# Two halves of 64 tokens solved in turn inside a chunk, the first clears on another queue, and a new order of turns

## The chip, the cores and the metric

The kernel runs on one core of a Trainium2 chip. Five engines work side by side, each with its own instruction stream that is executed in order: TensorE (PE: products and transposes, results into PSUM), VectorE (DVE), ScalarE (ACT), GpSimd (POOL) and SyncE (SP, which here only issues DMAs). The metric is the device time of one execution in microseconds; of several executions the median counts.

## The reference

The program is one layer in three parts on an input of 2 sequences x 4096 tokens x 256 features. All is float32.

```
x = x + 0.5 * ffn(layernorm(x))       # 8 experts, the best 2 of each token
x = x + attn(layernorm(x))
x = x + 0.5 * ffn(layernorm(x))
```

The expert part computes logits, a softmax over 8 experts, takes the two best, scales the token by each score, and adds `(silu(xs @ w1[e]) * (xs @ w3[e])) @ w2[e]` over those experts.

The attention has 4 heads of 64 and is a gated delta rule. For each chunk of tokens, with the state S carried from chunk to chunk:

```
A   = I + tril(Kb @ K.T, -1)          # Kb = K * beta
T   = inverse(A)                      # lower triangular
mid = T @ Vb - (T @ Kb) @ S.T
O   = Q @ S.T + (Q @ K.T * M) @ mid   # M: lower triangular ones
S   = S + mid.T @ K
```

Chunks of any length give the same result; the reference uses 64 tokens, the kernel 128. In block form, with A cut in two halves of 64, the low half of mid is T_ll r_l, and the high half is T_hh (r_h - A_hl mid_l), where r is the right side before T is applied. The change is about these two ways to get mid.

## The kernel before

**The units.** The tokens are cut in 16 units of 512 (256 of each sequence). The first expert layer handles them in groups of 1, 3, 4, 4, 4 units, the second in groups of 4, 4, 4, 3, 1. A group of one unit ("dense") runs all experts on all its tokens (`weigh`, `all_experts`). The other groups sort tokens by expert: `route` finds scores and slots, `scatter` puts each scaled token row into the DRAM buffer `slots` by an indirect DMA on GpSimd, `experts` reads pairs of 128-row tiles from `slots` (tile `xi`), runs the selected expert and stores to `made` (tile `yo`), and `combine` gathers two rows a token from `made`. There are two `slots` buffers, used by the groups in turn, of 40 tiles of 128 rows at most. Rows that no token takes must be finite, so `clear` (line 707) writes zeros into each buffer once, 8 tiles (1 MB) a DMA, from the zeroed tile `XT[1]` (4 KB a partition before it takes its first real content).

**Attention.** `project` makes k, q and v of a unit (products `pj`, a short convolution in `cv`). `gram` makes the matrix L = K K.T of a chunk of 128 tokens for 8 pairs of sequence and head, and stores its four diagonal blocks of 32 to DRAM. `substitute` inverts all 32-blocks of four chunks (128 rows at once) on VectorE, and stores the inverses X and their transposes. `inverse` (line 1359) puts the inverse of a chunk together:

- it loads the four 32-blocks of the transposed inverse into the diagonal of `xt` and three blocks of the inverse into `xx`, seven DMAs on SyncE;
- it joins blocks of 32 to blocks of 64 in both halves at once: products `pp`, negated copy `pm`, products `px`, copies back to `xt`; for the low half the untransposed corner is made as well (the third loop of `px`, copied into `xx`);
- it joins the two blocks of 64 to one of 128: products `pq` (L's corner times the high block), negated copy `pw`, products `pz` (times the low block), and a copy into the corner of `xt`.

`advance` (line 1409) then makes the masked product `at`, the transposed k (`kt`) and r; takes `pks` = K S off r; forms `pmid` = T r as eight products with 128 rows and 128 columns of weights; copies it to `mid`; and from mid makes the output `po` and the step of the state `pds`, which is added to S. `finish` normalises the output, applies Wo and stores. There are 32 chunks, one behind the other through S.

**PSUM.** Four rings of two banks: "fa" (projection, first expert products), "tr" (transposes), "at" (all of `inverse`, `gram` and `pa`), and "y" (`pks`, `pmid`, `po`, `pds`, the experts' second product `py`, and small ones). The tiles of a ring are handed out in the order of the program text.

**The order.** Nothing is issued while the program text runs: every operation is noted in `Plan.ops` with a cost, and `Plan.order` (line 432) then lays out all operations engine by engine with those costs. Among ready operations an engine takes the one with the lowest `first` value, which is the operation's number plus an entry of `TURNS` (line 47; one integer for a step of the program, a few thousand at most). `plan.together()` makes one operation of several products. `nc.either.copy` leaves it to this layout whether VectorE or ScalarE copies. `plan.hold` makes an operation wait, in this layout only, for a given earlier one. What is laid out becomes the real in-order streams of PE, DVE, ACT and SP. A `yield` in the program text ends a step and tells its estimated share.

**The head.** The first DMAs load x for the first unit, the experts' weights and further x. The second group (three units, `groups[1]`) gets its `slots` cleared by four DMAs on ScalarE's queue (line 1065) without a hold; the attention's weights follow on SyncE, held until `groups[0].last`, the operation that completes the dense group's weights `wt`. The other groups' clears (six DMAs) are on SyncE, held until `groups[1].last`.

Of the kernel before, what the change touches and what calls it, by code (L numbers as in the profile page):

```python
# [36 lines left out]
F32 = mybir.dt.float32  # L37
# [3 lines left out]
ALU = mybir.AluOpType  # L41
# [6 lines left out]
    0: -503, 1: -513, 2: -516, 3: -370, 4: -583, 5: 726, 6: -2518, 7: -130, 8: -302, 9: 87,  # L48
    10: -124, 11: -210, 12: -120, 13: -49, 14: -31, 16: 37, 17: 151, 18: 3947, 19: 159, 20: 180,
    21: 1716, 22: 88, 23: -235, 24: -40, 25: 1464, 26: 884, 27: 1522, 28: 483, 29: 1766, 30: 2462,  # L50
    31: 2582, 32: 3382, 33: 170, 34: -217, 35: 428, 36: -1592, 37: 115, 38: 51, 39: 255, 40: 643,
    41: -669, 42: -210, 43: -509, 44: 505, 45: -127, 46: 91, 47: 1585, 48: 38, 49: 1295, 50: 193,
    51: 1197, 52: 216, 53: -416, 54: 1088, 55: -982, 56: -953, 57: -958, 58: -1515, 59: -1356,
    60: -824, 61: -627, 62: -312, 63: -308, 64: -221, 65: -302, 66: -280, 67: -44, 69: -15,
    70: -62, 71: -145, 72: -50, 73: -46, 74: -1795, 75: -55, 76: -9, 77: 1, 78: 364, 79: 100,
    80: -128, 81: 123, 82: 108, 83: 111, 84: -136, 85: -35, 86: 81, 87: 3, 88: 209, 89: 883,
    90: -104, 91: -82, 92: -14, 93: -22, 94: 222, 95: 298, 96: 1362, 97: 420, 98: -2033, 99: 760,
    100: -48, 101: 25, 102: -85, 103: -2631, 104: -2008, 105: -27, 106: -111, 107: -2148,
    108: 1154, 109: -39, 110: -3637, 111: -2138, 112: -1132, 113: -2221, 114: 21, 115: -1517,
    116: -206, 117: -1803, 118: -1354, 119: -431, 120: -706, 121: 262, 122: -274, 123: -46,  # L60
    124: -191, 125: -192, 126: 422, 127: 1624, 128: 282, 129: 476, 130: -367, 131: 348,
    132: -1154, 133: -780, 134: 44, 135: -614, 136: -460, 137: -333, 138: 67, 139: -480,
    140: -469, 141: -1054, 142: -358, 143: -626, 144: 622, 145: -369, 146: -360, 147: -255,
    148: 396, 149: -432, 150: -147, 151: -170, 152: -32, 153: -7, 154: -43, 156: -10, 157: 68,
# [487 lines left out]
def kernel(  # L552
# [488 lines left out]
    def prepare(g):  # L1041
# [16 lines left out]
        for i in range(n):  # L1058
# [5 lines left out]
            if g is groups[1]:  # L1064
                clear(g.par, upto, nc.scalar)
                if i == 0:
                    plan.hold = groups[0].last
                    load_attention()
                    plan.hold = None
# [623 lines left out]
```

## Time and profile before

| | us |
|---|---|
| median of 9 executions | 1844.44 |
| lowest, highest | 1836.61, 1853.97 |
| the profiled execution's own time | 1850.08 |
| its span, first to last instruction | 1848.3 |
| PE busy | 1627.6 |
| VectorE busy | 1237.4 |
| ScalarE busy | 754.5 |
| GpSimd busy | 702.3 |
| first product of a chunk (`pp`) starts | 386.6 |
| last step of the state (`pds`) ends | 1718.3 |
| bytes moved | 259.48 MB, 140 GB/s in the mean |

How to read the lines of a profile: "L202 PE MATMUL pmid<-r,XT 128*128 128x64 f32 x512 | 69.7, 294 | 15.4 <-..." is a group of instructions: source line (L202 is a helper that records the operation, so the tile names tell which it is), engine, operation, output and inputs, weights' rows*columns, the moving operand's shape, the number; then busy us of all, ns of one; then the idle time of the engine just before them and what ended it. A float32 product leaves two records, so 512 are 8 products in each of 32 chunks. Suffixes a and b name the first and second expert layer's tiles or, in the attention, a unit's. In a timeline the first two numbers are start and length in us; a bracket tells idle time before and what released it. ACTq, SPq and POOLq are the issues of DMAs by ScalarE, SyncE and GpSimd. "PE" busy counts modelled ends of pipelined products; "PEld" are weight loads.

### The profile page before, as it was taken

How to read it: one execution, taken by the hardware profiler on the slowest of the kernel's cores; microseconds unless marked ns; L12 is line 12 of the kernel's file. 1: busy time of each engine (PE TensorE's matmuls, PEld its weight loads, DVE VectorE, ACT ScalarE, POOL GpSimd, SP SyncE). 2: the span in 40 equal slices, each digit the busy share in tenths (PEclk: the TensorE clock that was granted, in tenths of full speed). 3: DMA queues.
4: the chain of work that ended last, by engine and by line, in shares of the span. 5: the costliest groups of instructions: out<-in, count | busy, mean ns of one | idle time of the engine just before them, and what ended most of it. 6: DMA issues, size and time to landing. Idle time of an engine off the chain costs nothing.

```text
span 1848.3 us, 34449 instructions
## 1 busy us (share of the span) xinstructions
PE 1627.6 (88%) x11656; PEld 1234.3 (67%) x11656; DVE 1237.4 (67%) x4166; ACT 754.5 (41%) x1566; POOL 702.3 (38%) x800
## 2 busy tenths in 40 slices
PE   3978789689989989999999899789899989999898
PEld 2656466567667667667677677657676767777776
DVE  3637568775785786587956867876875868376344
ACT  1425435333343535343544435343443533334432
POOL 2413744453112322642333362332215423454434
PEclk9999989888999989998999999899899998999999
DMA  7173564554133235643332562342145535574774
GB/s 239 55 281 115 174 213 144 185 166 125 54 91 91 79 94 159 175 135 110 112 95 87 162 178 92 107 122 68 46 136 170 162 115 161 175 223 157 219 222 120
DMA packets 296396, 259.48 MB, mean 140 GB/s; under 512 B 117536, under 2 KB 275232, under 8 KB 296224
## 3 DMA queue, kind: packets, MB, share of 16 engines
q1 hardware_dynamic: 271552, 190.13, 34.0%
q0 software_dynamic: 23040, 62.95, 10.4%
q10 hardware_dynamic: 1632, 4.21, 0.6%
q8 instruction: 96, 1.57, 0.4%
q14 instruction: 76, 0.62, 0.1%
HBM read 137.52 MB, written 119.67 MB: 139 GB/s over the span
## 4 chain that ended last, share of the span: by engine, by line
PE 44%; DVE 20%; DMA 17%; issue 9%; ACT 5%; POOL 4%; SPq 2%; POOLq 0%; DVEq 0%; ACTq 0%
PE pj_a L202 5%; PE po L202 4%; DVE cv_a L202 4%; DMA got_b<-made,sli_b 3%; DMA got_a<-made,sli_a 3%; PE pb_a L202 3%; PE p_b L1109 3%; PE p_a L1109 3%; PE pmid L202 2%; POOL slots L934 2%; DMA slots<-row_a,sli_a 2%; PE py_a L1109 2%; DMA slots<-row_b,sli_b 2%; PE pyo L202 2%; PE py_b L1109 2%
## 5 line engine op out<-in xcount | busy, mean ns | idle before, releaser
L202 DVE SCALAR_TENSOR_TENSOR cv_a<-pre_a,cw_sb,cv_a 128x512 f32<-128x512 f32 x288 | 212.2, 744 | 7.2 <-ACT cv_a L223 3.8
L202 PE MATMUL pj_a<-xT_a,wp_sb 128*128 128x512 f32 x384 | 195.3, 612 | 8.0 <-DVE xT_a L217 3.1
L934 POOL DMA_INDIRECT slots<-row_b,sli_b x120 | 120.8, 1007 | 192.7 <-DVE sli_b L202 78.0
L1109 PE MATMUL p_a<-wx_sb,xiT_a 128*128 x608 | 160.2, 401 | 17.6 <-ACT xiT_a L218 8.0
L934 POOL DMA_INDIRECT slots<-row_a,sli_a x120 | 120.8, 1007 | 116.0 <-issue 39.1
L952 POOL DMA_INDIRECT got_b<-made,sli_b x120 | 117.1, 975 | 118.1 <-DMA made<-yo_b 21.4
L1109 PE MATMUL p_b<-wx_sb,xiT_b 128*128 x608 | 155.5, 389 | 5.7 <-ACT xiT_b L218 2.1
L952 POOL DMA_INDIRECT got_a<-made,sli_a x120 | 123.1, 1026 | 83.5 <-DVE x_a_1c L202 17.9
L1109 PEld LDWEIGHTS p_a<-wx_sb,xiT_a 128*128 128x128 f32 x608 | 115.5, 200 | 48.9 <-ACT xiT_a L218 14.3
L1109 PEld LDWEIGHTS p_b<-wx_sb,xiT_b 128*128 128x128 f32 x608 | 109.5, 191 | 28.7 <-ACT xiT_b L218 7.5
L1109 PE MATMUL py_a<-wx_sb,hT_a 128*128 x304 | 85.9, 403 | 10.9 <-DVE hT_a L217 4.6
L202 PEld LDWEIGHTS pj_a<-xT_a,wp_sb 128*128 128x128 f32 x384 | 64.8, 192 | 41.4 <-issue 23.9
L202 POOL TENSOR_TENSOR rs_a<-ve_a,mhalf 128x4 f32<-128x4 f32 x32 | 33.9, 1060 | 152.0 <-DVE ve_a L202 151.8
L202 POOL TENSOR_TENSOR rr<-ms,mhalf 128x8 f32<-128x8 f32 x32 | 54.4, 1699 | 93.3 <-DVE ms L202 93.0
L1109 PE MATMUL py_b<-wx_sb,hT_b 128*128 x304 | 85.0, 400 | 3.4 <-DVE hT_b L217 1.0
L202 PE MATMUL po<-mid,at 128*128 128x64 f32 x512 | 85.2, 296 | 3.2 <-DVE at L202 1.7
L202 POOL COPY pre_a<-carry 128x6 f32<-128x6 f32 x96 | 28.3, 296 | 156.2 <-DVE cv_a L202 132.5
L202 DVE TENSOR_TENSOR yb<-yb,z 128x31 f32<-128x31 f32 (+15 forms) x248 | 84.0, 339 | 4.5
L202 PEld LDWEIGHTS po<-mid,at 128*128 128x128 f32 x512 | 81.1, 224 | 8.0 <-ACT mid L218 3.9
L202 DVE TENSOR_TENSOR z<-lb,yb 128x31 f32<-128x31 f32 (+15 forms) x248 | 83.4, 336 | 4.2
L202 POOL COPY carry<-pre_a 128x6 f32<-128x6 f32 x96 | 28.3, 302 | 150.2 <-ACT pre_a L218 140.4
L202 PE MATMUL pmid<-r,XT 128*128 128x64 f32 x512 | 69.7, 294 | 15.4 <-issue 6.5
(290 smaller groups left out, 3877.9 us busy)
## 6 DMA issues: line engine op xcount, KB each, us to landing
xi_a<-slots SPq DMA_DIRECT2D x76, 256.0 KB
made<-yo_a SPq DMA_DIRECT2D x76, 256.0 KB
xi_b<-slots SPq DMA_DIRECT2D x76, 256.0 KB
made<-yo_b SPq DMA_DIRECT2D x76, 256.0 KB
x_a<-in_L_attn_x_dram SPq DMA_DIRECT2D x32, 256.0 KB
x_a<-mid SPq DMA_DIRECT2D x16, 512.0 KB
xr<-mid SPq DMA_DIRECT2D x64, 128.0 KB
mid<-xr SPq DMA_DIRECT2D x64, 128.0 KB
```

Source lines behind the costliest of these rows:

```text
L202: self.plan.add(self.name, lambda: real(*args, **kw), ins, outs, cost)
L934: ins = tc.nc.gpsimd.indirect_dma_start(out=dst, out_offset=bass.IndirectOffsetOnAxis(ap=slot, axis=0), in_=row, in_offset=None,)
L952: return tc.nc.gpsimd.indirect_dma_start(out=got, out_offset=None, in_=src, in_offset=bass.IndirectOffsetOnAxis(ap=slot, axis=0),)
L1109: return tc.nc.tensor.matmul(o, lhsT=lhsT, rhs=wx_sb.rearrange("p e c -> p (e c)")[:, cols], start=start, stop=stop,)
```

## The change

Four things are changed together.

1. `inverse` stops at blocks of 64. The products `pq` and `pz`, the third loop of `px`, and the copies `pw`, `XT<-pz` and `X<-px` go; one of the seven loads goes. The tiles `XT` and `X` are half as wide, as they hold the two blocks of 64 below each other.
2. `advance` applies the two blocks in turn: the low half of `mid` from the low half of r, then the product `pl` of L's corner with it, which is taken off the high half of r on VectorE, then the high half of `mid`. Each is a group of eight products of 64 rows by 64 columns of weights with 64 moving columns. `pl` and the second `pmid` take tiles of the "y" ring. L is read here and no longer in `inverse`, so six instead of four tiles of L are kept.
3. All clears are issued by SyncE; those of the second group are held until the first group's weights are complete, as the attention's weights are. The zeros come from a tile of half the width, so a row of a clear is 2 KB and no longer 4 KB.
4. `TURNS` is another table (1003 entries for steps 0 to 1022, where there were 1020 for 0 to 1054, since each of the 32 `inverse` calls has one step fewer). The mean size of an entry is 1141 where it was 617, the largest 7426 where it was 3947.

```diff
 TURNS = {
-    0: -503, 1: -513, 2: -516, 3: -370, 4: -583, 5: 726, 6: -2518, 7: -130, 8: -302, 9: 87,
...
+    1017: -173, 1019: -53, 1020: 16, 1021: -506, 1022: -372,
 }
...
-    XT = [const.tile([P, NH, P], F32, name=f"XT_{i}") for i in range(2)]
-    X = [const.tile([P, NH, 2 * XB], F32, name=f"X_{i}") for i in range(2)]
+    XT = [const.tile([P, NH, 2 * XB], F32, name=f"XT_{i}") for i in range(2)]
+    X = [const.tile([P, NH, XB], F32, name=f"X_{i}") for i in range(2)]
...
-    def clear(i, upto, engine):
+    def clear(i, upto):
         for t in range(cleared[i], upto, 8):
             n = min(8, upto - t)
-            engine.dma_start(
-                slots[i][t * P : (t + n) * P, :].rearrange("(p c r) d -> p c (r d)", p=P, r=4),
-                XT[1].rearrange("p h c -> p (h c)").unsqueeze(1).to_broadcast([P, n // 4, NH * P]),
+            nc.sync.dma_start(
+                slots[i][t * P : (t + n) * P, :].rearrange("(p c r) d -> p c (r d)", p=P, r=2),
+                XT[1].rearrange("p h c -> p (h c)").unsqueeze(1).to_broadcast([P, n // 2, NH * 2 * XB]),
             )
...
-            if g is groups[1]:
-                clear(g.par, upto, nc.scalar)
-                if i == 0:
-                    plan.hold = groups[0].last
-                    load_attention()
-                    plan.hold = None
-            else:
-                plan.hold = groups[1].last
-                clear(g.par, upto, nc.sync)
-                plan.hold = None
+            plan.hold = groups[0 if g is groups[1] else 1].last
+            clear(g.par, upto)
+            if g is groups[1] and i == 0:
+                load_attention()
+            plan.hold = None
...
-        l = blk.tile([P, BP, 2, P], F32, tag="L", name=f"L_{n}_{t}", bufs=4)
+        l = blk.tile([P, BP, 2, P], F32, tag="L", name=f"L_{n}_{t}", bufs=6)
...
-        xt, xx, l = XT[t % 2], X[t % 2], Ls.pop((n, t))
+        xt, xx, l = XT[t % 2], X[t % 2], Ls[n, t]
         for c in range(NC):
             s = ts(t * NC + c, NH)
             nc.sync.dma_start(
-                xt[ts(c, XB), :, ts(c, XB)], XTd[n % 2][s, :].rearrange("q (r c) -> r q c", c=XB)
-            )
-            if c < 3:
+                xt[ts(c, XB), :, ts(c % 2, XB)],
+                XTd[n % 2][s, :].rearrange("q (r c) -> r q c", c=XB),
+            )
+            if c % 2 == 0:
...
-                    mm(px[a][fst[a], q, :], xx[fst[a], q, 0:XB], pm[fst[a], q, :])
-            for q in range(NH):
-                mm(px[0][snd[0], q, :], pm[fst[0], q, :], xx[fst[0], q, 0:XB])
-        nc.either.copy(xx[snd[0], :, 0:XB], px[0][snd[0]])
+                    mm(px[a][fst[a], q, :], xx[fst[a], q, :], pm[fst[a], q, :])
         for a in range(2):
-            nc.either.copy(xt[fst[a], :, snd[a]], px[a][fst[a]])
+            nc.either.copy(xt[fst[a], :, XB:], px[a][fst[a]])
         yield 3.0
-        lo, hi = slice(0, 2 * XB), slice(2 * XB, P)
-        pq = ps.tile([P, NH, 2 * XB], F32, tag="at", name=f"pq_{v}")
-        with plan.together():
-            for q in range(NH):
-                mm(pq[lo, q, :], l[hi, q, lo], xt[hi, q, hi])
-        pw = wk.tile([2 * XB, NH, 2 * XB], F32, tag="pw", name=f"pw_{v}", bufs=1)
-        nc.either.copy(pw, pq[lo], -1.0)
-        pz = ps.tile([P, NH, 2 * XB], F32, tag="at", name=f"pz_{v}")
-        with plan.together():
-            for q in range(NH):
-                mm(pz[lo, q, :], xx[lo, q, :], pw[:, q, :])
-        nc.either.copy(xt[lo, :, hi], pz[lo])
-        yield 2.0
...
-        pmid = ps.tile([P, NH, D], F32, tag="y", name=f"pmid_{v}")
-        with plan.together():
-            for h in range(NH):
-                mm(pmid[:, h, :], XT[t % 2][:, h, :], r[:, h, :])
+        xt, l = XT[t % 2], Ls.pop((n, t))
+        lo, hi = slice(0, 2 * XB), slice(2 * XB, P)
         mid = wk.tile([P, NH, D], F32, tag="mid", name=f"mid_{v}", bufs=1)
-        nc.either.copy(mid, pmid)
+        for s in (lo, hi):
+            if s == hi:
+                pl = ps.tile([P, NH, D], F32, tag="y", name=f"pl_{v}")
+                with plan.together():
+                    for h in range(NH):
+                        mm(pl[hi, h, :], l[lo, h, hi], mid[lo, h, :])
+                nc.vector.tensor_tensor(r[hi], r[hi], pl[hi], ALU.subtract)
+            pmid = ps.tile([P, NH, D], F32, tag="y", name=f"pmid_{v}_{s.start}")
+            with plan.together():
+                for h in range(NH):
+                    mm(pmid[s, h, :], xt[s, h, :], r[s, h, :])
+            nc.either.copy(mid[s], pmid[s])
```

## The prediction

> **What bounds the kernel now.** I read the page first, then a table of four stages (cut at the first and the last instruction of the chunks' products), then the groups by shape, then the timeline of single chunks and of the head.
>
> ```profile
> PE 1627.6 (88%) x11656; PEld 1234.3 (67%) x11656; DVE 1237.4 (67%) x4166; ACT 754.5 (41%) x1566; POOL 702.3 (38%) x800
> PE 44%; DVE 20%; DMA 17%; issue 9%; ACT 5%; POOL 4%; SPq 2%; POOLq 0%; DVEq 0%; ACTq 0%
> ```
>
> PE is the busiest engine, yet the chain of waits that ended last lies on it for 44% only, so I look stage by stage (columns: busy us of PE, PEld, DVE, ACT, POOL; granted clock; DMA share; GB/s).
>
> ```profile
> 0.00:100.00 100.00, 65.87 (x283) 47.08 (x284) 49.09 (x265) 29.80 (x73) 34.38 (x55) 0.98 0.41 143
> 100.00:377.00 277.00, 221.40 (x1040) 159.14 (x1039) 182.34 (x775) 117.79 (x248) 122.00 (x135) 0.93 0.58 189
> 377.00:1720.00 1343.00, 1227.32 (x9777) 939.17 (x9778) 950.06 (x2964) 562.42 (x1139) 489.23 (x553) 0.95 0.42 126
> 1720.00:1848.30 128.30, 113.05 (x559) 88.88 (x557) 55.95 (x166) 44.47 (x106) 56.70 (x58) 1.00 0.60 185
> ```
>
> All 32 chunks lie in the third stage. There PE is busy for 1227.32 of 1343 us (91%), DVE 71%, ACT 42%, DMA 42%: this stage is PE's. 115.7 us of PE idleness remain in it. In the head PE is idle for a third of 100 us, so something else sets the time there.
>
> The recurrence through S has room. Chunk 18 issues pks at 1124.93, pmid at 1131.06, pds at 1137.19 and is done at 1138.30; the next pks starts at 1177.0. A lap from pks to the end of pds takes 8.5 to 14 us for most chunks, 1343 / 32 = 42 us are there for each.
>
> **The products, chunk by chunk.** Busy time of matmuls overlaps at the ends, so I price a group by the distance from its start to the start of what PE does next (timeline, us and length):
>
> ```profile
> 806.25 1.97 PE L202 MATMUL pmid<-r,XT 128*128 128x64 f32 x16
> 808.06 0.44 PE L202 MATMUL po<-S,q 128*128 128x128 f32 x2
> ...
> 828.33 0.57 PE L202 MATMUL px<-X,pm 32*32 32x32 f32 x13
> 828.83 0.44 PE L202 MATMUL phs_a<-ident,hs_a 128*128 128x128 f32 x2
> ...
> 829.86 1.14 PE L202 MATMUL pq<-XT,L 64*64 64x64 f32 x16
> 830.93 1.99 PE L1109 MATMUL p_a<-wx_sb,xiT_a 128*128 x8
> ```
>
> pmid 1.81, the third part of px 0.50 (its last 13 of 16 records), pq 1.07. pz is of pq's shape and costs 1.07 too. Over all chunks the medians are 1.84, 0.50, 1.07, 1.07. Removed: 1.84 + 0.50 + 1.07 + 1.07 = 4.48. Added: the low pmid, pl and the high pmid, three groups of eight products of 64x64 by 64 columns, pq's shape: 3 x 1.07 = 3.21. Net -1.27 a chunk, x 32 = **-41 us**, on the engine that bounds this stage. From busy times by group it would be (69.7 + 22.3 + 37.2 + 39.5) - 3 x 38.4 = 53; I take the smaller.
>
> [...] The change makes three 64x64 stretches a chunk where there were two. [...]
>
> **The hand-overs.** What leaves: px -> X -> pq, pq -> pw -> pz, pz -> XT. What comes, on the recurrence: low pmid -> mid -> pl, and pl -> r -> high pmid. One hand-over, bare:
>
> ```profile
> 391.70 1.14 PE L202 MATMUL pq<-XT,L 64*64 64x64 f32 x16
> ...
> 392.98 0.58 ACT L223 ACTIVATE pw<-pq 64x512 f32<-64x512 f32 x1
> ...
> 393.82 1.14 PE L202 MATMUL pz<-pw,X 64*64 64x64 f32 x16
> ```
>
> From 392.84 to 393.82 it is 0.98 us; through DVE (a 64x512 subtraction as long as r's of 128x512, 0.68) about 1.0, as from pks to pmid where nothing lies between (0.8 to 1.1 in the closest chunks). PE has other work in most of these:
>
> ```profile
> L202 PE MATMUL po<-mid,at 128*128 128x64 f32 x512 | 85.2, 296 | 3.2 <-DVE at L202 1.7 <-ACT mid L218 1.0
> L202 PE MATMUL pmid<-r,XT 128*128 128x64 f32 x512 | 69.7, 294 | 15.4 <-issue 6.5 <-DVE r L202 5.5 <-DVE z L202 3.3
> L202 PE MATMUL pz<-pw,X 64*64 64x64 f32 x512 | 39.5, 232 | 0.6 <-ACT pw L223 0.2
> L202 PE MATMUL pq<-XT,L 64*64 64x64 f32 x512 | 37.2, 224 | 5.6 <-ACT XT L218 3.5 <-DVE XT L217 1.6 <-issue 0.3
> ```
>
> The two present hand-overs on the recurrence left PE idle for 15.4 + 3.2 = 18.6 us in all, 0.29 us each. Two more: +19. The ones that go had 5.6 + 0.6: -6. Net **+13 us**; bounds -6 (all covered) and 2 x 1.0 x 32 - 6 = +58 (none). I take the rate of the present ones, whose neighbours are the same. The cover is the experts' and the projection's products. Its limit is the ring of two "y" banks, given out in program order: between pks and pds no expert product can leave through py, and two more tiles (pl, the second pmid) now stand in that row. A lap grows by 2 x 1.0 + 3 x 1.07 - 1.84 = 3.4 us. PE can meanwhile do the two p13 that "fa" holds, and transposes.
>
> DVE gains a 0.68 us subtraction, and together DVE and ACT lose three copies and gain one: about 22 us more for DVE in the stage at worst, from 71% to 72%: 0, hidden behind PE. SyncE issues 32 X loads fewer (64 for 96), out of hundreds: 0. XT comes free only after the high pmid, some 4 us later; SyncE waited for pmid 19.1 us in 10 cases, so its queue, with xi loads and made stores behind those waits, may stand 40 us longer in total. PE's waits for xi loads are only 18.4 us in all: 0, at most +6. L lives until pl, but the two additional buffers are just what the next pair of chunks takes: 0.
>
> **The head.** (SPq and ACTq are the DMA issues of SyncE and ScalarE.)
>
> ```profile
> 6.17 18.54 ACTq L202 DMA_DIRECT2D slots<-XT  x4
> 26.03 0.59 ACT L218 COPY xT_a<-ptx_a 128x512 f32<-128x512 f32 x1
> 26.67 3.78 PE L202 MATMUL plt_a<-xT_a,wg_sb 128*128 128x512 f32 x4 [15.85 <-ACT xT_a L218]
> ...
> 30.24 0.37 SPq L202 DMA_DIRECT2D x_a<-in_L_attn_x_dram  x1
> 31.64 3.51 PE L202 MATMUL p_a<-wx_sb,xT_a 128*128 128x256 f32 x8
> ...
> 98.75 0.89 SPq L202 DMA_DIRECT2D xi_a<-slots  x2
> ```
>
> ScalarE is held until 24.7 by the four clears, the copy of the first xT stands behind them, and PE waits 15.9 us for it. With the clears on SyncE that copy can run at 11.5, the logits by 16, and the first p_a by 17.5 if the experts' weights are there. They and the first x are 4.2 MB; at the first slice's 239 GB/s that is 17.5 us, so about 20 with the landing: p_a some 11.6 us earlier. The clears, held until the first group's weights are made (about 24 then), take SyncE's queue where it issues nothing from 30.6 to 98.75. Their 4.2 MB need 17.5 us, so they land by about 45, ahead of the first scatter (61.7, less 11.6). If this cover fails, the first scatter waits for two clears: 8.8 + 2.9 = +12. Bounds -15.9 and +12. I take **-8**, two thirds of 11.6, since what follows to 98.75 runs through DVE and GpSimd as well. Rows of 2 KB in place of 4 KB: 0; the six later clears go with one 6.8 us wait for xi, which at worst doubles.
>
> [...]
>
> **The order.** New turns move every engine's order; no row prices that. A better order can at most fill the 115.7 us; a worse one could lose as much. I put 0, and half of it either way only in the rivals.
>
> **Sum.** -41 + 13 - 8 = -36. The profiled execution took 1850.08 (span 1848.3), 5.6 above the median: 1814 for it, 1844 - 36 = **1808** as a median. Its own bounds: 1844 - 41 - 6 - 15 = 1782 and 1844 - 41 + 35 + 0 = 1838.
>
> **Rivals.**
> - *Deeper gain*, 0.15: hand-overs covered (-6), the head's 11.6 kept in full, and the order fills a quarter of the idle 115.7 (-29): 1844 - 41 - 6 - 12 - 29 = 1756. For it: 91% busy leaves that room. Against: a longer recurrence is harder to fill.
> - *Slower, through the y ring*, 0.25: both new hand-overs lie open (+64 - 6) since the expert stream dries up while pks to pds holds the ring, and for a fifth of the 3.4 us x 32 longer laps PE stands after them too (+22): 1844 - 41 - 8 + 58 + 22 = 1875. It decides once more than 49 us of idleness come in. For it: pmid has the largest sum of waits among the chunk's groups. Against: 25 to 40 us between laps.
> - *The relief isn't used*, 0.08: the freed 41 us turn into idleness as scatters, gathers and DVE set the pace: 1844 - 8 = 1836 to 1848. Against: none is over 71%.
>
> Forecast: 0.52. Faster by over 0.5% (about what a measurement of this kernel tells from no change): the forecast and the deeper gain, 0.66; within it 0.09; slower 0.25. The range goes from 1770, which leaves out half of the deeper gain, to 1868, which takes in the milder part of the slower rival.
>
> **What would show it.** After: PE busy in the third stage less by 40 to 55 us; pmid in 64x64 form at 1.07 a group; idleness before pl and the high pmid under 20 us in all; the first plt near 12 and p_a near 20; SyncE's clears ahead of the scatters. I am wrong if idleness before pl, the high pmid or py exceeds 50 us, or if PE's idle share in the third stage grows over 11%.

## The result and the profile after

The changed kernel takes 1866.78 us (median of 20 runs, 1858.72 to 1875.58) where the kernel before takes 1848.21 on the same chip (62 runs): a ratio of 1.0106, 95% interval 1.0089 to 1.0123. It is **1.1% slower**; 2% faster was forecast. Executions more than 1.5% above the fastest of their kernel are left out of every ratio and mean. The profiled execution has a span of 1864.8 us, against 1848.3 before.

Busy times and the shares of the chain of waits, from the page of the kernel after:

```profile
PE 1632.4 (88%) x11144; PEld 1233.6 (66%) x11144; DVE 1249.4 (67%) x4163; ACT 735.8 (39%) x1537; POOL 702.0 (38%) x800
PE 45%; DVE 22%; DMA 17%; issue 7%; ACT 5%; POOL 3%; SPq 1%; POOLq 0%; ACTq 0%; DVEq 0%
```

PE issues 512 matmul records fewer and yet is busy 5 us longer. The four stages of the kernel after, at the cuts used before (us from and to, length, busy us of PE, PEld, DVE, ACT and POOL, granted clock, DMA share, GB/s), say where that is from:

```profile
0.00:100.00 100.00, 76.77 (x336) 55.85 (x336) 52.31 (x270) 32.96 (x81) 33.02 (x55) 0.95 0.61 210
100.00:377.00 277.00, 225.68 (x1051) 158.57 (x1052) 188.96 (x777) 115.96 (x250) 125.11 (x141) 0.90 0.55 173
377.00:1720.00 1343.00, 1202.79 (x9117) 916.08 (x9111) 947.36 (x2940) 536.68 (x1091) 480.45 (x539) 0.91 0.41 122
1720.00:1848.30 128.30, 115.71 (x606) 94.44 (x603) 55.17 (x162) 46.61 (x106) 60.18 (x63) 0.99 0.62 193
```

The head does more (76.77 us of PE work in the first 100 us, 65.87 before). In the third stage the granted clock is 0.91; it was 0.95. The records of the clock in the two profiles have two values only, 1 and 0.5, so a stage's half-clock time can be added up. Where PE is busy in it, I count half of that busy time as lost, an estimate from one kind of product (sixteen of 64x64 took 3.67 us in a stretch whose clock was 0.51, and at the 0.117 us each that they took at 1.00 they would take 1.87, in the runs of products alone below); where PE is idle in it, I count nothing. With the chunk stage cut at its own ends, from the first pp to the last pds, its length falls into three parts: PE idle, the time lost to the clock by this count, and the rest, which is PE's work as it would be at full clock.

| us | before | after | difference |
|---|---|---|---|
| start to first pp | 386.6 | 375.1 | -11.5 |
| chunk stage | 1331.7 | 1353.4 | +21.7 |
| - PE idle | 113.0 | 140.8 | +27.8 |
| - lost to the clock (half of PE's busy time at half clock) | 61.1 | 98.1 | +37.1 |
| - work at full clock | 1157.6 | 1114.4 | -43.2 |
| time at half clock, PE busy or idle | 139.9 | 232.1 | +92.2 |
| last pds to the end | 129.9 | 136.4 | +6.5 |

The work that was to go did go. More than all of it came back: 27.8 us as idleness and 37.1 as a slower clock. PE's groups in the kernel after, by shape (busy us, mean ns, idle us before them and who ended it):

```profile
L203 PE MATMUL po<-mid,at 128*128 128x64 f32 x512 | 94.3, 319 | 4.1 <-ACT mid L219 2.4 <-DVE mid L218 1.4 <-DVE at L203 0.2
L203 PE MATMUL pmid<-r,XT 64*64 64x64 f32 x1024 | 84.3, 241 | 24.8 <-DVE r L203 21.2 <-ACT XT L219 3.0 <-DVE XT L218 0.5
...
L203 PE MATMUL pl<-mid,L 64*64 64x64 f32 x512 | 41.9, 241 | 7.8 <-ACT mid L219 6.2 <-DVE mid L218 1.6
...
L203 PE MATMUL pp<-XT,L 32*32 32x32 f32 x1024 | 25.7, 200 | 19.1 <-DMA XT<-XTd 18.3 <-DVE at L203 0.6
```

Two things are to be seen. po is untouched by the change, and its mean record went from 296 to 319 ns, with the stage's clock at 0.91 for 0.95. And pp, which hardly waited (3.1 us), now waits 19.1:

```profile
L202 PE MATMUL pp<-XT,L 32*32 32x32 f32 x1024 | 23.4, 194 | 3.1 <-DMA XT<-XTd 1.9 <-DVE at L202 1.2
```

That is before. After, most of the wait falls in one place, in chunk 4 (timeline of PE after, start and length):

```profile
518.42 1.89 PE L1105 MATMUL p_a<-wx_sb,xiT_a 128*128 x8
535.64 0.31 PE L203 MATMUL pp<-XT,L 32*32 32x32 f32 x2 [15.33 <-DMA XT<-XTd]
```

The solve of these four chunks is stored at 526.89 and its pieces are loaded behind that; PE has nothing else standing there. Before, the store came at 541.15, pp at 547.96, and PE had projections, expert products and transposes in between. From 524.4 to 558.5, beyond the end of the wait, the clock was at half:

```profile
524.40:558.50 34.10, 21.43 (x230) 19.65 (x232) 7.01 (x18) 4.25 (x10) 2.58 (x2) 0.50 0.21 51
```

The head after, on ScalarE, PE and SyncE:

```profile
9.29 0.58 ACT L219 COPY xT_a<-ptx_a 128x512 f32<-128x512 f32 x1 [5.82 <-PE ptx_a L203]
...
9.93 2.07 PE L203 MATMUL plt_a<-xT_a,wg_sb 128*128 128x512 f32 x2 [0.25 <-ACT xT_a L219]
11.80 0.90 PE L203 MATMUL p_a<-wx_sb,xT_a 128*128 128x256 f32 x2
...
16.07 1.29 SPq L203 DMA_DIRECT2D slots<-XT  x2
```

The first expert product is at 11.80 (31.64 before), the clears begin behind it, and the first scatter is issued at 41.44 (61.72 before). So 20 us were gained up to there; 11.5 of them are left at the first pp.

### The profile page after: what moved, and what is told of

The parts are those of the page before. It is cut to its first block, busy times and chain, and to the rows that moved or that the text cites. A ratio compares the mean times of both kernels' runs of the same rounds, so it can differ in the third digit from the quotient of the medians.

```text
span 1864.8 us, 33379 instructions
## 1 busy us (share of the span) xinstructions
PE 1632.4 (88%) x11144; PEld 1233.6 (66%) x11144; DVE 1249.4 (67%) x4163; ACT 735.8 (39%) x1537; POOL 702.0 (38%) x800
## 3 DMA queue, kind: packets, MB, share of 16 engines
q0 software_dynamic: 23040, 62.95, 10.6%
## 4 chain that ended last, share of the span: by engine, by line
PE 45%; DVE 22%; DMA 17%; issue 7%; ACT 5%; POOL 3%; SPq 1%; POOLq 0%; ACTq 0%; DVEq 0%
DMA got_b<-made,sli_b 5%; PE po L203 4%; DVE cv_a L203 4%; PE pj_a L203 4%; PE p_a L1105 4%; DMA got_a<-made,sli_a 3%; PE pb_a L203 3%; PE p_b L1105 3%; PE pmid L203 2%; PE py_a L1105 2%; PE py_b L1105 2%; DMA slots<-row_b,sli_b 2%; DVE yb L203 2%; DMA slots<-row_a,sli_a 2%; DVE z L203 2%
## 5 line engine op out<-in xcount | busy, mean ns | idle before, releaser
L203 PE MATMUL pj_a<-xT_a,wp_sb 128*128 128x512 f32 x384 | 192.1, 609 | 11.5 <-ACT cv_a L224 2.6
L1105 PE MATMUL p_a<-wx_sb,xiT_a 128*128 x608 | 163.3, 409 | 13.8 <-ACT xiT_a L219 7.3
L953 POOL DMA_INDIRECT got_b<-made,sli_b x120 | 117.3, 977 | 117.1 <-DVE hT_b L218 16.6
L953 POOL DMA_INDIRECT got_a<-made,sli_a x120 | 121.5, 1013 | 82.8 <-issue 19.5
L1105 PE MATMUL py_a<-wx_sb,hT_a 128*128 x304 | 93.0, 426 | 18.0 <-issue 5.2
L203 PE MATMUL pmid<-r,XT 64*64 64x64 f32 x1024 | 84.3, 241 | 24.8 <-DVE r L203 21.2
L203 PEld LDWEIGHTS pmid<-r,XT 64*64 64x64 f32 x1024 | 74.8, 153 | 45.3 <-DVE r L203 28.9
L203 PE MATMUL po<-mid,at 128*128 128x64 f32 x512 | 94.3, 319 | 4.1 <-ACT mid L219 2.4
L203 PEld LDWEIGHTS po<-mid,at 128*128 128x128 f32 x512 | 89.7, 246 | 10.0 <-ACT mid L219 5.7
L1105 PE MATMUL py_b<-wx_sb,hT_b 128*128 x304 | 84.9, 396 | 5.1 <-DVE S L203 2.0
L219 ACT COPY pre_a<-pj_a 128x512 f32<-128x512 f32 x86 | 50.3, 585 | 80.1 <-PE pj_a L203 62.1
```

Of the source, the lines that this page charges most:

```text
L203: self.plan.add(self.name, lambda: real(*args, **kw), ins, outs, cost)
L219: lambda: nc.scalar.copy(out, in_),
L953: return tc.nc.gpsimd.indirect_dma_start(out=got, out_offset=None, in_=src, in_offset=bass.IndirectOffsetOnAxis(ap=slot, axis=0),)
L1105: return tc.nc.tensor.matmul(o, lhsT=lhsT, rhs=wx_sb.rearrange("p e c -> p (e c)")[:, cols], start=start, stop=stop,)
```

## The experiments

Three theories were stated at first. **CLOCK**: PE is slowed to half in stretches that hold mostly small products. **ORDER**: the new turns are a worse order. **RING**: the two more tiles of the "y" ring hold up those behind them. Later ones are named where they come up. All runs but the last two fell on slower chips, where the kernel before takes 1906 to 1920 us; every ratio is to the kernel before on the same chip. There the pair of kernels differs as above: chunk stage 1379.0 and 1407.0 us (profiles c1_before and c2_after, the two kernels once more; c2_after: ratio 1.0077, 1.0041 to 1.0114). "The control" is c2_after.

A profile shows one execution, and the clock differs from one execution to the next. So the table gives, beside the profile's parts of the chunk stage (us, as above), the mean granted clock of the whole span, first in the profiled execution, then over all executions of the run and over those of the kernel before on the same chip (their number in brackets).

| run | idle | lost to clock | work | at half clock | clock, profiled | clock, mean | before, mean |
|---|---|---|---|---|---|---|---|
| c1_before | 128.4 | 90.9 | 1159.7 | 194.6 | 0.933 | - | 0.932 (10) |
| c2_after | 163.2 | 126.2 | 1117.5 | 293.5 | 0.905 | 0.906 (8) | 0.931 (22) |
| e1, before, no turns | 146.7 | 117.3 | 1155.6 | 252.6 | 0.911 | 0.920 (4) | 0.935 (14) |
| e2, after, no turns | 179.3 | 136.5 | 1112.5 | 314.0 | 0.902 | 0.898 (4) | 0.935 (14) |
| e7c, one tile | 166.7 | 120.6 | 1117.4 | 283.3 | 0.906 | 0.904 (6) | 0.932 (10) |
| e11b, hand-overs cut | 167.7 | 115.8 | 1117.2 | 279.9 | 0.904 | 0.910 (10) | 0.931 (22) |
| e14, long wait gone | 161.2 | 104.0 | 1119.7 | 238.9 | 0.917 | 0.909 (12) | 0.932 (21) |
| e9, pmid 128 rows | 176.8 | 86.9 | 1124.5 | 211.6 | 0.922 | 0.918 (10) | 0.931 (22) |
| e6, pl wide as well | 151.2 | 99.8 | 1145.9 | 232.1 | 0.922 | 0.917 (5) | 0.935 (14) |
| e16, e14 and e9 at once | 171.3 | 105.0 | 1121.1 | 241.6 | 0.916 | 0.917 (12) | 0.932 (21) |
| e15, wide product added | 163.3 | 121.1 | 1134.5 | 286.7 | 0.905 | 0.911 (7) | 0.932 (21) |
| e18, po split | 141.2 | 94.9 | 1124.1 | 228.7 | 0.921 | 0.922 (6) | 0.952 (17) |
| e17, before, clears moved, split | 127.5 | 65.0 | 1148.3 | 146.8 | 0.949 | 0.946 (12) | 0.952 (17) |
| e8, before, halves apart | 152.7 | 84.9 | 1144.0 | 194.6 | 0.934 | 0.936 (9) | 0.935 (14) |
| e10, before, clears moved | 129.0 | 80.5 | 1162.7 | 177.5 | 0.938 | 0.936 (5) | 0.932 (10) |

Within one kernel the clock of single executions spreads by 0.002 to 0.006 (standard deviation), so a difference of 0.01 between two means is clear and one of 0.002 is not.

**The order.** Both kernels without fitted turns.

```diff
-TURNS = { 0: -503, ... }
+TURNS = {}
```

> The kernel before with an empty table of turns: every operation keeps its own place in the program text as its rank. Only the order differs from before. Three theories of why the change lost time: CLOCK (the products of 64x64 keep PE less active, and the granted clock falls), ORDER (the table found anew makes a worse order on the chip than the old one did), RING (the two more tiles on the y ring and the two more hand-overs leave PE idle). This run is one half of a pair with the next one. All theories: slower than before, 1880 to 1980 us, since the table was worth something; granted clock 0.91 to 0.95.

> The changed kernel with an empty table of turns; to be set against the kernel before without turns, so that neither has a fitted order. ORDER: faster than that one by 25 to 45 us, as 41 us of products and some 10 us of the head went. CLOCK: within 15 us of it, with a granted clock lower by 0.02 to 0.04 and PE's idle time about the same. RING: slower than it by 10 us or more, PE idle for 50 us more between the chunks' first and last product, the clock much the same.

Before without turns: 1.0266 (1.0205 to 1.0327). After without turns: 1.0322 (1.0276 to 1.0367). Where neither has a fitted order the change still gains nothing, so ORDER as the whole cause falls. The pattern is the same too: work -43 us, idle +33, half-clock time +61, and by the means the clock is 0.022 lower. CLOCK expected that fall and a time within 15 us (it is 6), but not the idleness. The long wait is there as well, before the first pp of chunk 4 (e2, timeline):

```profile
537.48 0.31 PE L83 MATMUL pp<-XT,L 32*32 32x32 f32 x2 [12.92 <-DMA XT<-XTd]
```

pp's longest wait in e1 is 3.6 us. So the wait comes with the change even where no turns were fitted.

**The y ring.** pl and both halves of pmid in one tile, the order of every engine kept as it was.

```diff
-pl = ps.tile([P, NH, D], F32, tag="y", name=f"pl_{v}")
-mm(pl[hi, h, :], l[lo, h, hi], mid[lo, h, :])
+mm(pmid[hi, h, :], l[lo, h, hi], mid[lo, h, :])   # pmid: one tile for all three
```

> The changed kernel with pl and both halves of pmid in one PSUM tile (pl takes the upper rows until the subtraction has read them), so that a chunk takes one slot of the y ring for them as before the change and not three; every engine's order as it was, nothing left out. RING (the prediction's slower rival: the two more tiles a chunk hold up those behind them): idle time of the chunk stage falls by 15 us or more and the kernel is 15 to 45 us faster than the changed kernel, ratio 0.985 to 1.003 to the kernel before. CLOCK: nothing waits on that ring that matters: ratio 1.006 to 1.013, idle time within 10 us of the changed kernel's.

Ratio 1.0111 (1.0062 to 1.0160), idle 166.7, clock 0.904: no gain over the changed kernel. RING falls, and with it the mechanism of the prediction's slower rival.

**The hand-overs.**

```diff
-mm(pl[hi, h, :], l[lo, h, hi], mid[lo, h, :])
+mm(pl[hi, h, :], l[lo, h, hi], r[lo, h, :])
-nc.vector.tensor_tensor(r[hi], r[hi], pl[hi], ALU.subtract)
+nc.vector.tensor_tensor(mid[hi], r[hi], pl[hi], ALU.subtract)
```

> The changed kernel with its two added hand-overs cut: pl reads r's lower half instead of mid's, and the subtraction of pl writes to mid's upper half, which the second pmid product no longer waits for, so that all three product groups can start once r is there; every engine's order as it was. What mid holds is then not the reference's. HAND-OVERS: PE's idle time in the chunk stage falls by 25 to 40 us, the half-clock time falls with it by 30 us or more, and the kernel is 35 to 60 us faster than the control, below the kernel before by 1% or more. CLOCK: idle time falls by 10 to 30 us, the half-clock time stays within 25 us of the control's, and the kernel is 5 to 30 us faster than the control, 0.995 to 1.008 of the kernel before.

Ratio 1.0028 (1.0002 to 1.0053), 6 us under the control. pmid's idle time fell from 27.5 to 10.6 us and pl's from 9.1 to 2.1, but the stage's didn't fall (167.7 for 163.2), since po took up part of the wait (11.5 us for 4.8). The subtraction still comes ahead of the copy into mid's upper half, and po waits for that copy, so the chain is shorter here but not gone:

```profile
L203 PE MATMUL po<-mid,at 128*128 128x64 f32 x512 | 94.6, 319 | 11.5 <-ACT mid L219 6.3 <-DVE mid L218 4.6 <-issue 0.3
```

The HAND-OVERS theory (35 to 60 us) doesn't hold as far as this run cuts them; CLOCK's figure for the time held, its figure for the idleness (10 to 30 us less) did not.

**The long wait.** Chunk 4's loads take the group's solve before, ahead of the new stores.

```diff
+old = made[0][s, :].rearrange("q (r c) -> r q c", c=XB)
+real = old if (n, t) == (1, 0) else src       # and issued ahead of Xd's store
-nc.sync.dma_start(dst, src)
+nc.sync.dma_start(dst, real)
```

> The changed kernel without the one long wait of its chunk stage (15.3 us before the first pp of chunk 4, in every profile of the changed kernel so far): the six loads of chunk 4's XT and X read the solve of the group of chunks before, and stand ahead of the new solve's stores on SyncE; what chunk 4 is solved with is then not the reference's; every other order as it was. STALL (the wait is the largest single piece of the loss, and its place is also where the clock goes down): idle time of the chunk stage 12 to 20 us less than in the changed kernel, half-clock time 10 to 40 us less, 15 to 32 us faster, ratio 0.993 to 1.002. RIVAL (the stage gives it back: what chunk 4 no longer waits for, the next solve's results or the clock take): less than 8 us faster, ratio 1.004 to 1.012.

Ratio 1.0053 (1.0023 to 1.0084): inside the rival's range (1.004 to 1.012), outside STALL's. The profile alone looks better: the stage is 22 us shorter than in the control, with 55 us less at half clock and only 2 us less idleness. But the profiled execution had the highest clock of its twelve (0.917); their mean is 0.909, 0.023 under the kernel before, where the control is 0.025 under it. So most of the 55 us is that execution's luck. In chunk 4 itself the half clock lasted 34.1 us in the control and 20.5 here (537.8 to 558.3), where PE's longest wait was 2.3 us; it lasted 20.5 us in e9 too, where the long wait is still there. The wait's idleness was taken up in part by others (px waits 16.1 us for 11.9). That the long wait is what holds the clock down is not shown.

**Products alone.** Does the clock follow the kind of product, or PE's idleness? First without gaps:

```diff
+for i in range(n):
+    for a, c in zip(rows, cols):
+        mm(o[c, j : j + wide], w[a, c], r[a, j : j + wide])
```

> Not the kernel: product groups alone on TensorE, nothing for them to wait for, one kind in each stretch of 30 to 70 us and wide products (128x128 by 256) between the stretches; none of the reference is computed. Kinds in order: 64x64 with 64 in the free size in one half; the same in both halves in turn; 128x128 by 64; 128 rows to 64 columns by 64; 32x32 by 32; transposes of 128x128; 128x128 by 512. [...] BUSY (rival: the gate looks at busy time alone, and the half clock of the kernel comes from idle time): every stretch is granted full clock throughout.

CLOCK is half right here: 64x64 products without a gap held full clock (1.00 over 59 us), and of the seven kinds only 32x32 by 32 fell (0.54), at 97% busy (one execution; columns as above; no ACT there):

```profile
24.00:83.00 59.00, 59.00 (x1015) 59.00 (x1014) 0.00 (x0) 0.00 (x0) 1.00 0.07 24
...
284.00:339.00 55.00, 53.29 (x2005) 52.10 (x1998) 0.00 (x0) 0.00 (x0) 0.54 0.02 4
```

Then with gaps. In a first form wide products slid into the gaps, so that only its last stretches can be used:

> Not the kernel: laps of products on TensorE, each lap's first product waiting for a VectorE copy of the lap before, with 24 or 32 laps of one kind in a stretch and wide products between the stretches; none of the reference is computed. Kinds in order: 16 of 64x64 by 64; 16 of 128 rows to 64 columns by 64; 8 of 128x128 by 64; 4 of 128x128 by 256 (all near 1.8 us of products a lap), then 8 of 64x64, 4 of 128x128 by 64 and 2 of 128x128 by 256 (near 0.9 us a lap). CLOCK (the gate weighs what the products use of the array, not busy time alone): at one and the same gap the 64x64 laps fall to half clock and the 256 wide ones of 1.8 us hold full clock; 128 rows to 64 columns lies between. BUSY (rival): the laps of 1.8 us are all granted alike, and those of 0.9 us alike, whatever the product.

and in a second the order was held:

```diff
+for k in range(n):
+    mm(o[c, j : j + wide], w[a, c], last[a, j : j + wide])
+nc.vector.tensor_scalar_mul(last[c, :], o[c, :], 0.05)
```

> Not the kernel: laps of products on TensorE in the order written, each lap's products reading a VectorE copy of the lap before, so that PE sits idle for some 0.5 to 1.2 us between laps; 24 or 32 laps of one kind in a stretch, 24 wide products without a gap between the stretches; none of the reference is computed. Kinds in order: half (16 of 64x64 by 64), rows (16 of 128 rows to 64 columns by 64), full (8 of 128x128 by 64), wide (4 of 128x128 by 256), all near 1.8 us of products a lap at full clock; then half, full and wide with half as many. CLOCK (the gate weighs what the products do, not busy time alone): the half laps fall to half clock while the wide laps of the same length hold full clock, with rows and full between; of the short ones half and full fall. BUSY (rival): the four kinds of 1.8 us are granted alike, and so are the three short ones.

Every gap is 0.51 or 0.52 us. In the order half, rows, full, wide, then short half, full, wide (the clock is the third number from the end):

```profile
32.60:130.80 98.20, 86.43 (x768) 81.97 (x768) 16.57 (x47) 0.00 (x0) 0.51 0.00 1
143.90:205.50 61.60, 49.90 (x768) 46.57 (x768) 16.54 (x47) 0.00 (x0) 1.00 0.01 2
217.20:315.60 98.40, 86.50 (x384) 82.04 (x384) 9.76 (x23) 0.00 (x0) 0.51 0.00 0
330.20:389.90 59.70, 47.81 (x192) 34.47 (x192) 9.76 (x23) 0.00 (x0) 1.00 0.00 0
401.60:478.80 77.20, 61.42 (x512) 55.47 (x512) 22.19 (x63) 0.00 (x0) 0.52 0.00 1
492.00:568.60 76.60, 60.54 (x256) 54.62 (x256) 13.15 (x31) 0.00 (x0) 0.53 0.00 1
583.00:635.20 52.20, 36.14 (x128) 21.63 (x128) 13.15 (x32) 0.00 (x0) 1.00 0.00 0
```

By their means the four that fell had some 2 to 5 us at full clock (an estimate: 0.51 of 98.2 us and 0.53 of 76.6 us). Of the laps with some 1.9 us of products at full clock (an estimate from 0.117 us for one of 64x64), with one and the same gap, 64x64 by 64 and 128x128 by 64 ran at half clock nearly throughout (0.51), 128 rows to 64 columns and 256 wide products at full (1.00). BUSY falls: the 64x64 laps are busy for 88% of their stretch at half clock, and would be for some 78% at full (an estimate: 16 x 0.117 of 2.39 us), yet they fell, while what is busy for 69% (the last line) ran at full. CLOCK doesn't come out whole either: it had rows and full between the two, but rows, with weights of 128x64, held (1.00), and full, with weights of 128x128, fell (0.51). What the clock counts is not found; it is one stretch of each kind, in one execution. Two wide products a lap with the same gap, in the first form, ran at half clock for all of their 82 us:

```profile
460.00:542.40 82.40, 66.38 (x128) 37.59 (x128) 13.17 (x31) 0.00 (x0) 0.50 0.00 0
```

So laps of the same two products and the same gap ran at 1.00 in one run and at 0.50 in the other; what decides between the two is not shown. For the kernel two things follow. The product that left, pmid in 128x128 by 64, is of a kind that fell there (0.51), just as the 64x64 that came in its place (0.51); and the change has three 64x64 groups a chunk where there were two, and one group of 128x128 by 64 less. So the kinds by themselves don't say why the changed kernel's clock is lower.

Are the waits the cause? In chunk 4 of the kernel after, the half clock begins 4.1 us after the start of the 15.3 us wait (524.4 and 520.31); in e14 chunk 4 falls to half clock too (at 537.8), with waits of 2.3 us at most. So in that execution it took no such wait.

**The kind of product in the kernel.** pmid's halves summed over 128 rows of XT and r instead of 64, in the second run pl wide as well.

```diff
-mm(pmid[s, h, :], xt[s, h, :], r[s, h, :])
+mm(pmid[s, h, :], xt[:, h, :], r[:, h, :])
-mm(pl[hi, h, :], l[lo, h, hi], mid[lo, h, :])    # e6 only
+mm(pl[:, h, :], l[lo, h, :], mid[lo, h, :])
```

> The changed kernel with one edit: the two pmid products of a chunk are summed over all 128 rows of XT and r instead of the half's 64, every engine's order as it was. What mid holds is then not the reference's. A pmid group should still take 1.07 us, since its columns and its free size are the same, so PE's work doesn't change. CLOCK (PE is slowed to half in stretches filled with small products, which count less towards the granted clock than wide ones): the half-clock time of the chunk stage falls from 232 to 170-215 us and the kernel is 8 to 30 us faster than the control. HAND-OVERS (the added waits are what costs, the clock only follows them): same as the control within 6 us, half-clock time within 15 us.

> The changed kernel, every engine's instructions in the very same order, but its narrow products widened: both halves of pmid sum over all 128 rows (so mid is not the reference's; the other half's rows are added in), and pl uses all 128 columns of L as weights (its low half is not read). Same number of products and of moving columns. CLOCK: granted clock back from 0.919 to 0.935 to 0.95, time 15 to 35 us below the changed kernel (1866.8), unless the wide groups themselves are longer, which their start-to-start distance (1.07 us now) will tell. ORDER and RING: the clock stays within 0.01 and the time within 6 us, but for longer groups.

e9: ratio 1.0030 (0.9993 to 1.0068), 10 us under the control beside it; work +7 us, half-clock time 211.6 (-82), idle 176.8 (+14). Over all executions the clock is 0.918 for 0.906. pmid's mean record hardly changed, 245 ns for 243 in the control, though it has twice the rows (e9, by shape):

```profile
L732 PE MATMUL pmid<-r,XT 128*64 128x64 f32 x1024 | 84.5, 245 | 38.9 <-DVE r L203 27.0 <-ACT XT L219 4.4 <-DVE x_b_1c L203 2.2
```

e6: its wide pl takes 1.925 us a group for 1.07, 27 us more work, and the kernel stands at 1.0104 (1.0069 to 1.0140), no slower than the changed kernel; its half-clock time is 232.1 and its mean clock 0.917, on another chip than the control. By the means e9 is 0.013 and e6 0.018 under the kernel before on the same chip; the unwidened c2_after, e7c, e11b, e14 and e15 are 0.021 to 0.028 under it. So the clock was higher with wider sums in pmid, as CLOCK expected; HAND-OVERS, which expected the half-clock time to stay, falls again.

Both at once, the long wait gone and 128 rows:

> The run with the long wait gone, and both pmid products summed over 128 rows as well; chunk 4's solve and what mid holds are not the reference's. If the stall and the clock are two separate pieces of the loss, their gains add: 8 to 15 us below the run with the wait gone alone, ratio 0.985 to 0.998, faster than the kernel before by some 10 us, which the head alone would give. RIVAL (both are the same piece, since the clock falls where PE waits): no more than 4 us below the run with the wait gone alone.

Ratio 1.0022 (0.9988 to 1.0056), 3 us under the run with the wait gone alone, which is within the spread. The mean clock is 0.917 for 0.909, so it is higher with the wider sums here too (their profiles alone, 241.6 and 238.9 us at half clock, hide that), but hardly any time comes of it. Whether two gains add can't be told where the first one was not there.

More tries to raise the clock, or to take work out, inside the kernel:

```diff
+mm(pl[:, 0:4, :], l[:, 0, :], l[:, 1:3, :])      # e15: a wide product ahead of pl
-mm(po[:, h, :], at[:, h, :], mid[:, h, :], False, j == 1)
+for c in (lo, hi):                                # e18; in e17 pmid as well, and the clears moved
+    mm(po[c, h, :], at[:, h, c], mid[:, h, :], False, j == 1)
-mm(pmid[:, h, :], XT[t % 2][:, h, :], r[:, h, :])
+for a in halves:                                  # e8, on the kernel before
+    mm(pmid[a, h, :], XT[t % 2][a, h, a], r[a, h, :])
```

> The changed kernel with useless work added: one product of 128x128 by 256 ahead of each chunk's pl group, into pl's tile before pl's own products are written over it; nothing else changed. It takes 0.44 us at full clock, 14 us over 32 chunks. CLOCK: half-clock time of the chunk stage falls by 25 to 90 us, and the kernel is 8 us slower to 25 us faster than the changed kernel. WORK (rival: PE's busy time is what counts and half clock has another cause): half-clock time within 20 us of the changed kernel's, the kernel 8 to 20 us slower than it.

> The changed kernel with po's 512 products of 128x128 by 64 split in the same way; order and results as in the changed kernel. CLOCK: half-clock time of the chunk stage 40 to 110 us less than in the changed kernel on a chip of this speed (293 us), ratio 0.985 to 1.003. RIVAL (waits take it back): ratio 1.003 to 1.010.

> The kernel before with the clears moved, and each product of 128x128 by 64 of pmid and po (mid with at) split into two of 128 rows to 64 columns, which in the run with gaps took the same time and kept full clock where the unsplit ones did not; order and results as before. CLOCK: PE's work stays (the split pair takes what the one took), the half-clock time of the chunk stage falls by 40 to 110 us against the run with the clears moved alone (177 us there), and the kernel is another 8 to 40 us faster: ratio 0.970 to 0.986. RIVAL (what the clock gives, PE's waits take back): half-clock time falls but idle time rises by nearly half as much; ratio 0.986 to 0.996. RIVAL (the twice as many instructions cost what the clock gives): PE's work in the stage is up by 15 us or more, ratio 0.990 to 1.005.

> The kernel before, every engine's instructions in the same order, but each of pmid's eight products of 128x128 weights is made as two of 64x64, low and high half by themselves (the corner of the inverse is left out, so mid is not the reference's). No new wait and no new tile. The groups get longer by about 0.3 us (16 products of 64x64 at 0.134 against 8 of 128x128 at 0.23), x 32 = 10 us. CLOCK: the granted clock falls from 0.95 by 0.01 to 0.03 and the time rises by 20 to 35 us. ORDER and RING: the clock stays, +10 us at most.

e15: 1.0111 (1.0061 to 1.0161), half-clock time 286.7, work +17: CLOCK's 25 to 90 us did not come. WORK's figure for the clock held; its 8 to 20 us of time can't be told from the 1 to 7 measured.

e18: 1.0137 (1.0096 to 1.0177), outside both ranges and no faster than the changed kernel; half-clock time 228.7, as without the split (232.1 us in the kernel after).

e17: 0.9968 (0.9940 to 0.9995), half-clock time 146.8 for 139.9, idle 127.5 for 113.0 (both against the profile before); its ratio is that of the third case expected, but its work is down by 9 us (1148.3) and not up, so none of the three fits. What the products alone showed, 1.00 for 128 rows to 64 columns where 128x128 by 64 had 0.51, did not carry over to po.

e8 takes 16 us of work out of the kernel before and puts 64x64 in the place of 128x128 by 64, without a new wait. CLOCK expected a lower clock and 20 to 35 us more; the mean clock stayed (0.936 for 0.935) and the ratio is 0.9960 (0.9916 to 1.0004), so CLOCK falls here, and ORDER and RING's figure holds. In its profile the idle time rises by 24 us against c1_before: the work taken off PE came back as waiting.

**The head.** The kernel before with its four clears moved in SyncE's stream, nothing else.

```diff
 for k, e in order:                  # plan.late: the four clears
+order = [x for x in order if x[0] not in self.late]
+order[at:at] = late                 # behind groups[0].last, on nc.sync
```

> The kernel before with the change's third part alone: the four 1 MB clears of the head go from ScalarE's stream to SyncE's, behind the last step of the first group's placing; every engine's order is otherwise as before. HEAD (the part pays what the prediction gave it, and what comes behind keeps it): first chunk product 8 to 14 us earlier than in the kernel before, span 5 to 15 us shorter, ratio 0.992 to 0.997, faster than both kernels. RIVAL (the later stages take it back, as work that comes earlier meets the same clock and the same waits): ratio 0.998 to 1.003.

Ratio 0.9892 (0.9837 to 0.9946), faster than both kernels and more than HEAD expected (0.992 to 0.997). The first pp comes at 377.7, 19.5 us earlier than in c1_before, and the chunk stage kept it (1372.2 us for 1379.0). In e17, on another chip, the clears moved in the same way and the first pp came at 367.7, 18.9 us earlier than in the kernel before (386.6). ScalarE's copy (e10, timeline) no longer stands behind the clears:

```profile
10.43 0.58 ACT L219 COPY xT_a<-ptx_a 128x512 f32<-128x512 f32 x1 [6.96 <-PE ptx_a L203]
...
14.90 3.96 SPq L719 DMA_DIRECT2D slots<-XT  x4
```

## Why the prediction was wrong, step by step

- *The products, -41.* Right: 43 us of work at full clock (42 on the slower chip). The prices from start to start were the good ones; the 53 by busy times, which the prediction set aside, would have been too much. A group costs 1.07, where eight such products without a gap took 0.94 (59.9 us for 512): the two ends of a group cost 0.13 (an estimate from these two), and the price had it in.
- *The hand-overs, +13.* Right in size. pmid, pl and po have 24.8 + 7.8 + 4.1 = 36.7 us of idleness; pmid, po, pq and pz had 15.4 + 3.2 + 5.6 + 0.6 = 24.8 before: +12. Cutting them in part gave 6 us.
- *The head, -8.* Right in sign and small: -11.5. In the kernel before the same step gives 19; where the other 8 us are lost, by the new turns or otherwise, was not tried.
- *The order, 0.* pp's idleness grew by 16 us (19.1 for 3.1), the most visible part of the 28 beside the hand-overs; other groups gained and lost about as much. No term of the sum has this wait for the loads of the solved blocks. It needs neither the new turns (e2 has it without them) nor does it come with the clears moved alone (e10: pp waits 3.2 us in all), so what is left is the solve in two halves; how that makes it is not shown.
- *The missing term.* This is the step that failed: the sum takes 41 us of products off the stage's length as if each product left kept the clock of before, 0.95. At 0.91 the clock costs 37 us more than before (35 on the slower chip), as much as the whole gain that the sum promised (36).

With these the stage adds up: -43 + 12 + 16 + 37 = +22. The first plt and p_a were put near 12 and 20 and came at 9.93 and 11.80. The head's -11.5 and 6.5 us more at the end make some 16.5, the difference of the spans; the 6.5 are not explained.

Why the clock falls stays open. Wider sums in pmid bring back 0.008 to 0.012 of some 0.025 (e9, e16), a third to nearly a half, but the time follows only by 10 us and 3 us: in e9's profile the clock gives back 39 us, 14 of idleness and 7 of work come in, and the first pp is 4 later. The wider sums go with a higher clock, but they are not the reason that it fell: the kind that left fell as the kind that came did (0.51 for both in the run with gaps), and changing one for the other alone left the clock as it was (e8: 0.936 for 0.935). The y ring (e7c), the fitted turns (e2) and the long wait (e14) are not the cause by themselves; the hand-overs, as far as e11b cuts them, gave back 0.004. The clears moved alone don't lower the clock (e10: 0.936 for 0.932), so the fall, too, comes with the solve in two halves. Not tried is whether it is their sum, or the three small groups standing close together with short waits between them.

Of the signs named, PE's busy time in the third stage fell by 25 us and not 40 to 55, because busy time grows at half clock (3.67 us for 1.87 above); with each stage cut at its own ends it fell by 6 us, 43 less work and 37 more from the clock. Idleness before pl and pmid (32.6 us) lay between the 20 hoped for and the 50 that would have shown the slower rival. That rival's time, 1875, was nearest to the outcome, by luck: e7c excludes the ring by which it works, and it has no clock in it. The 1866.8 lies within the stated range, 1770 to 1868, only because the range was stretched to take in part of that rival; the direction was wrong.

## What to carry to other kernels

Before pricing work taken off TensorE, read the granted clock of the stage and put it into the sum as a term of its own with bounds: here the clock took back 37 of the 43 us that the products gave, and none of the tries on shapes, waits, ring and order explained more than a part. Cut a stage into idle time, half of PE's busy time at half clock and the rest, before and after; busy time alone hides all three. Read the clock over all executions before believing the one that was profiled: e14's profile showed a gain that the mean of its twelve executions does not have. And of a change in four parts try each alone: here one part, four DMA issues that held an engine for 18.5 us, was worth 1% by itself and was buried by the others.

## What the runs showed of the hardware

- 1024 records of 64x64 in one half took 59.9 us, the same number in both halves in turn 30.1 (the run without gaps). In e8 the 32 records of a pair of halves took 1.08 us (403.05 to 404.13), what 16 in one half took there (pq, 398.79 to 399.87):

```profile
403.05 1.15 PE L731 MATMUL pmid<-r,XT 64*64 64x64 f32 x32
404.13 0.49 PE L202 MATMUL po<-S,q 128*128 128x128 f32 x2
```

- Products of 128 rows to 64 columns took what those of 64x64 did (59.9 us for 1024 records, both, without gaps), and with gaps of 0.51 us they held full clock (1.00) where those fell (0.51).
- Laps of two wide products with gaps of 0.52 us ran at 1.00 for 52.2 us in the second run with gaps and at 0.50 for 82.4 us in the first.
- The kernel before takes 1848 and 1849 us where the main result and e17 ran and 1906 to 1920 on others, with 140 and 195 us at half clock in the chunk stage of its two profiles.
